# Rows that are transposed by way of DRAM and VectorE, and a start and a middle in another order, in a convolution and mixture-of-experts kernel

## The chip, the cores and the metric

The kernel runs on one core of a Trainium2 chip. Its time is the device time of one execution in microseconds (us); several executions are measured and their median is used. A profile is one execution recorded by the hardware profiler. PE is TensorE (PEld its weight loads), DVE is VectorE, ACT is ScalarE, POOL is GpSimd, and SP is the engine whose queue issues most of the transfers.

## The reference

Inputs are `x` and a context, both 8 x 256 x 512, one convolution filter of 512 taps for each of 32 heads, and the weights of a mixture of experts. Everything is float32.

```
def xattn(v, k, bias, x1, x2):                  # x1 = x2 = context
    kv = vr[:, :, :, None, :] * x2r[:, :, None, :, :]   # 8 x 8 products per head
    y  = causal_convolution(kv, k) + kv * skip          # along the 512 positions
    return einsum('bhijl,bhil->bhjl', y, x1r)
def ffn(xf):                                    # 2048 rows of 512
    scores = sigmoid(xf @ gate_w.T)             # 8 experts, the best 2 of each row
    shared = silu(xf @ shared_wg.T) * (xf @ shared_wu.T) @ shared_wd.T     # 704 wide
    routed = sum over the 2 best of 2.5 * weight * expert(xf)              # 352 wide
    return shared + routed
x = x + xattn(layernorm(x), ...)
x = x + ffn(layernorm(x), ...)
```

## The kernel before, in words

The 2048 rows are 16 tiles of 128 rows; a tile holds 16 channels of all 8 batches, which is two heads. The order of the work on every engine is written out by hand: each engine runs its instructions in the order in which the program issues them.

*Convolution stage.* The loop runs over the 32 heads `h`; `t = h // 2` is the tile. For a head, POOL makes the products `kv` (`make_kv`, two heads ahead), PE multiplies them with Toeplitz blocks of the filter (`conv_products`: ten 128x512 products into four PSUM tiles; three PSUM buffers are there), and DVE weighs each of the four results with the context and sums (`weigh(h, 0)` to `weigh(h, 3)`: a product and a reduction each). The skip term is made on POOL (`skip_products`, `skip_spread`) around a sum on DVE (`skip_sum`, `add_skip`).

`kv` needs the layer-normed tile with positions on the partitions, `vT`. DVE computes mean and variance (`stats`), ACT a square root (`rstd_of`), DVE the normed rows (`normed`); PE transposes them in four 128x128 pieces against an identity into PSUM and ACT copies them out (`transposed`, called by `make_vT`). A tile's finished sum is transposed back in the same way (`residual_T`) and added to `x` (`add_residual`). The result is normed a second time, written to DRAM as `xn_d` (for the experts' gathers later) by a transfer on SP, and transposed on PE into `xfT` (`make_xfT`), the operand of the shared expert. The odd heads do the norms of two tiles: `xn1` of tile t+2 and `xn2` of tile t-1. PE's transposes follow at the end of the same odd head.

*Shared expert and routing.* Four tiles form a chunk. Its shared products are cut into ten `steps` (six `up_step`, four `down_step`), which the head loop draws from head 10 on, one or two a head, at the end of the head; `settle` issues what they owe to DVE at the start of the next. Routing of a chunk is spread over heads: `route_logits` (PE), `route_T` (PE), `route_pick` (DVE), `route_ranks` (PE), `route_places` (DVE, then eight indirect writes on POOL into a table in DRAM).

*Tail and experts.* After the loop the last tile is normed and transposed, the last chunk is routed, the table is read back, and the remaining shared steps fill PE in between. Then 36 to 39 blocks of 128 gathered rows run through their experts. `block_T` there already brings a block into transposed form without PE: the rows are gathered in quarters, so that the 32x32-square transpose of DVE (`V.transpose`) gives a full transpose with the positions in a permuted order, and the weights' rows are permuted to match on the host.

*Start.* Tile 0 is normed, transposed, and its first `kv` made; tile 1 is normed and transposed; `kv` of head 1 and the skip products follow; then the head loop begins.

SP's queue holds all loads in program order: the Toeplitz block three heads ahead, `x` and context three tiles ahead, the residual's `x`, then whatever is written out. A transfer that waits there holds up those behind it.

Of the kernel before, what the change touches and what calls it, by code (L numbers as in the profile page):

```python
# [8 lines left out]
F32 = mybir.dt.float32  # L9
I32 = mybir.dt.int32  # L10
AF = mybir.ActivationFunctionType
ALU = mybir.AluOpType
# [28 lines left out]
Q = 32  # L41
NQ = P // Q
EPS = 1e-5
SCALE = 2.5


@with_exitstack
def tile_xattn_moe(
# [70 lines left out]
    load_toeplitz(1)  # L119


    ident = const.tile([P, P], F32, name="ident")
    make_identity(nc, ident)
    skip_sb = const.tile([P, D], F32, name="skip_sb")
# [10 lines left out]
    for e in range(NEXP):  # L135
        G.memset(rank[:, e : e + 1], float(NEXP - e))
        G.memset(base[:, e : e + 1], float(NTOK * e))
    ones = const.tile([P, P], F32, name="ones")
    G.memset(ones, 1.0)
    upper = const.tile([P, P], F32, name="upper")  # L140
    G.memset(upper, 1.0)

# [32 lines left out]


    xn_d = dram.tile([NTOK + P, L], F32, name="xn_d")
    NCOL = NEXP * CPE
    table = dram.tile([P * NCOL, 2], F32, name="table")
    zero = rows.tile([P, L], F32, tag="xg", name="zero")  # L180
# [26 lines left out]
    def rstd_of(mvs, n, m):  # L207
        r = small.tile([P, m], F32, tag="rstd", name=f"rstd{n}")
        V.tensor_scalar_add(r, mvs[:, :m, 1], EPS)
        A.activation(r, r, AF.Sqrt)  # L210
        V.reciprocal(r, r)
        return r

    def normed(tag, n, src, mv, r):
        xn = cvp.tile([P, L], F32, tag=tag, name=f"{tag}{n}", bufs=2)
        V.tensor_scalar(xn, src, mv[:, 0:1], r, ALU.subtract, ALU.mult)
        return xn

    def transposed(dst, src, n):
        pt = ps_tp.tile([P, NLB, P], F32, tag="tp", name=f"pt{n}")  # L220
        for k in range(NLB):
            T.transpose(pt[:, k, :], src[:, k * P : (k + 1) * P], ident)
        A.copy(dst, pt)  # L223
# [3 lines left out]
    def make_vT(t):  # L227
        vT[t] = cvp.tile([P, NLB, B, R], F32, tag="vT", name=f"vT_{t}")
        transposed(vT[t].rearrange("p k b r -> p k (b r)"), xn1.pop(t), f"v_{t}")

    def make_xfT(t):
        c, i = divmod(t, TPC)
        if i == 0:
            xfT[c] = shp.tile([P, NLB, TPC, P], F32, tag="xfT", name=f"xfT_{c}", bufs=2)
        transposed(xfT[c][:, :, i, :], xn2.pop(t), f"f_{t}")


    kvs = {}
# [34 lines left out]
    def weigh(h, lb, ps):  # L273
        t, cols = head_cols(h)
        if h % 2 == 0 and lb == 0:
            convT[t] = cvp.tile([P, NLB, B, R], F32, tag="conv", name=f"convT_{t}")
        prod = cvp.tile([P, B, NH, NH], F32, tag="prod", name=f"prod_{h}_{lb}", bufs=2)
        V.tensor_tensor(  # L278
            prod,
            ps,  # L280
            ctxT[t][:, lb, :, cols].unsqueeze(2).to_broadcast([P, B, NH, NH]),
            ALU.mult,
        )
        V.tensor_reduce(convT[t][:, lb, :, cols], prod, AX.X, ALU.add)  # L284
# [5 lines left out]
    def skip_products(t):  # L290
        if t >= NT:
            return
        s = cvp.tile([P, NLB, B, R], F32, tag="skip", name=f"skip_{t}")
        G.tensor_tensor(s, vT[t], ctxT[t], ALU.mult)
        flat = s.rearrange("p k b r -> p (k b) r")
        G.tensor_tensor(
            flat,
            flat,
            skip_sb[:, t * R : (t + 1) * R].unsqueeze(1).to_broadcast([P, NLB * B, R]),
            ALU.mult,  # L300
        )
        skips[t] = s

    def skip_sum(t):
        if t >= NT:
            return
        sums[t] = small.tile([P, NLB * B * 2], F32, tag="w", name=f"w_{t}")
        V.tensor_reduce(sums[t], skips[t].rearrange(BY_HEAD, i=NH), AX.X, ALU.add)

    def skip_spread(t):  # L310
        if t >= NT:
            return
        G.tensor_tensor(
            skips[t].rearrange(BY_HEAD, i=NH),
            ctxT[t].rearrange(BY_HEAD, i=NH),
            sums.pop(t).unsqueeze(2).to_broadcast([P, NLB * B * 2, NH]),
            ALU.mult,
        )
# [339 lines left out]
    def first_norms(ts):  # L658
        mv = small.tile([P, 2, V.BN_AGGR_DIM], F32, tag="mv", name=f"mvp_{ts[0]}")
        for n, t in enumerate(ts):  # L660
            stats(mv[:, n, :], f"p_{t}", x1[t])
        r = rstd_of(mv, f"p_{ts[0]}", len(ts))
        for n, t in enumerate(ts):
            xn1[t] = normed("xn1", f"_{t}", x1.pop(t), mv[:, n, :], r[:, n : n + 1])

    first_norms([0])
    make_vT(0)
    make_kv(0)
    first_norms([1])
    make_vT(1)  # L670
    make_kv(1)
    skip_products(0)

    todo = iter(steps)
    done = 0
# [1 line left out]
    def step():  # L677
        nonlocal done
        _, f, *a = next(todo)
        f(*a)  # L680
        done += 1

    def second_norm_of(t, mv, r):
        xn2[t] = normed("xn2", f"_{t}", x2[t], mv, r)
        S.dma_start(out=xn_d[t * P : (t + 1) * P, :], in_=xn2[t])

    for h in range(H):
        t, odd = divmod(h, 2)

        load_toeplitz(h + 3)  # L690
        if not odd:
            load_tile(t + 3)
            load_residual(t)
        if h == 3:
            load_shared()

        settle()
        pss = list(conv_products(h))
        weigh(h, 0, pss[0])
        ns = []  # L700
        if odd:
            skip_sum(t + 1)
            mvs = small.tile([P, 2, V.BN_AGGR_DIM], F32, tag="mv", name=f"mv_{h}")
            if t > 0:
                add_residual(t - 1)
                stats(mvs[:, len(ns), :], f"2_{t}", x2[t - 1])
                ns.append(("xn2", t - 1))
            if t + 2 < NT:
                stats(mvs[:, len(ns), :], f"1_{t}", x1[t + 2])
                ns.append(("xn1", t + 2))  # L710
            rs = rstd_of(mvs, f"_{h}", len(ns))
        else:
            if t == 0:
                skip_sum(0)
            else:
                add_skip(t - 1)
        weigh(h, 1, pss[1])
        for n, (tag, tt) in enumerate(ns):
            if tag == "xn2":
                second_norm_of(tt, mvs[:, n, :], rs[:, n : n + 1])  # L720
            else:
                xn1[tt] = normed(tag, f"_{tt}", x1.pop(tt), mvs[:, n, :], rs[:, n : n + 1])
        c, r = divmod(h - 10, 8)
        if c >= 0:
            if r == 2:
                route_pick(c)
            if r == 3:
                route_places(c)
        weigh(h, 2, pss[2])
        weigh(h, 3, pss[3])  # L730

        make_kv(h + 2)
        if not odd:
            skip_products(t + 1)
            skip_spread(t)

        if not odd and t > 0:
            residual_T(t - 1)
        if odd:
            if t > 0:  # L740
                make_xfT(t - 1)
            if t + 2 < NT:
                make_vT(t + 2)
        if c >= 0:
            if r == 0:
                route_logits(c)
            if r == 1:
                route_T(c)
            if r == 2:
                route_ranks(c)  # L750

        while done < min((h - 9) * 5 // 4, len(steps)) and steps[done][0] <= h:
            step()


    last_t, last_c = NT - 1, NCHUNK - 1
    settle()
    add_skip(last_t)
    step()
    residual_T(last_t)  # L760
    settle()
    add_residual(last_t)
    mvs = small.tile([P, 2, V.BN_AGGR_DIM], F32, tag="mv", name="mv_last")
    stats(mvs[:, 0, :], "2_last", x2[last_t])
    second_norm_of(last_t, mvs[:, 0, :], rstd_of(mvs, "_last", 1))
    step()
    make_xfT(last_t)
    conv_scope.close()
# [204 lines left out]
def _laid_out(a):  # L973

    import numpy as np

    toep = np.zeros((H, P, L), np.float32)
    for p in range(P):
        toep[:, p, p:] = a["L0_xattn_k"][:, : L - p]
    x = a["x"].reshape(B, NT, R, L).transpose(1, 0, 2, 3).reshape(NT, P, L)  # L980
    c = a["ctx_2048"].reshape(B, NT, R, NLB, P)

    g, u = a["L0_ffn_shared_wg"].T, a["L0_ffn_shared_wu"].T
    cols = [w[:, f : f + P] for f in range(0, SFF, P) for w in (g, u)]
    sgu = np.concatenate(cols, axis=1).reshape(NLB, P, 2 * SFF).transpose(1, 0, 2)
    gu = np.stack([a["L0_ffn_exp_wg"], a["L0_ffn_exp_wu"]], axis=1)

    gu = gu.reshape(NEXP, 2, FF, NQ, NLB, Q).transpose(0, 3, 5, 1, 4, 2)
    nf = len(F_TILES)
    squares = [q * nf + t for t in range(nf) for q in range(NQ) if q * nf + t < FF // Q]  # L990
    order = [s * Q + a for s in squares for a in range(Q)]
    return {
        "x": x,
        "cT": c.transpose(1, 4, 3, 0, 2),
        "toep": toep,
        "skip": a["fside_S2_0"],
        "gwT": a["L0_ffn_gate_w"].T,
        "sgu": sgu,
        "sd": a["L0_ffn_shared_wd"].T,
        "egu": gu.reshape(NEXP, P, NGU),  # L1000
        "ed": a["L0_ffn_exp_wd"].transpose(0, 2, 1)[:, order],
    }
# [24 lines left out]
```

## Time and profile before

| | us |
|---|---|
| median of 3 runs | 834.97 (834.58 to 836.86) |
| the profiled execution, whole | 848.52 |
| its span, first to last instruction | 846.8 |
| PE busy | 810.1 |
| DVE busy | 533.9 |
| POOL busy | 432.5 |
| ACT busy | 106.5 |

The profiled execution is longer than the others, so that its parts are compared with its own time. A busy PE is not PE at its peak, since matmuls overlap: the distance between starts tells what one holds of the engine. In groups of instructions, `x64` is the count, the next figures are the busy time and the mean duration. In a timeline the first figure is the start, the second the time covered, and a bracket gives the idle time before it and what ended it.

### The profile page before, as it was taken

What the parts mean: (1) busy time and instruction counts of PE and PEld (TensorE: products, weight loads), DVE (VectorE), ACT (ScalarE), POOL (GpSimd) and SP (SyncE); (2) the same over time, 40 slices, a digit from 0 to 9 for tenths busy, and PEclk for the clock granted to TensorE, in tenths of its full rate; (3) what the DMA queues carried; (4) which work ended last, traced back from release to release, by engine and by line L of the source; (5) the groups of instructions that cost most, each with busy time, mean ns of one, the idle gap of its engine ahead of it and who ended that gap; (6) DMA issues with size and microseconds to landing.
All of it is one profiled execution on the core that took longest, in us unless ns stands there. A gap on an engine that the chain in (4) does not pass through costs nothing. (4 is left out here: it accounts for less than half of the span.)

```text
span 846.8 us, 7786 instructions
## 1 busy us (share of the span) xinstructions
PE 810.1 (96%) x2247; PEld 399.2 (47%) x2247; DVE 533.9 (63%) x1340; ACT 106.5 (13%) x176; POOL 432.5 (51%) x424
## 2 busy tenths in 40 slices
PE   6999999999999999999999999979999999999991
PEld 3444444444444444444444444435555555555550
DVE  3888856657535757555555444309887788888860
ACT  1000111201011111002111010001111111111110
POOL 7965653194343074532341003762777777777521
PEclk9999999999999999999999999988999999999996
DMA  5372312201212011111000195229444444444332
GB/s 199 104 256 74 99 51 64 74 13 62 91 47 63 12 62 53 59 63 35 15 26 1 51 409 167 69 69 297 72 74 73 75 73 71 70 72 74 61 40 36
DMA packets 33418, 71.49 MB, mean 84 GB/s; under 512 B 6752, under 2 KB 7136, under 8 KB 32224
## 3 DMA queue, kind: packets, MB, share of 16 engines
q1 hardware_dynamic: 22560, 52.06, 17.9%
q0 software_dynamic: 10816, 18.92, 13.0%
q8 instruction: 20, 0.33, 0.2%
q14 instruction: 22, 0.18, 0.1%
HBM read 52.45 MB, written 18.51 MB: 84 GB/s over the span
## 5 line engine op out<-in xcount | busy, mean ns | idle before, releaser
L264 PE MATMUL cv<-kv,tz 128*128 128x512 f32 x640 | 282.3, 596 | 0.0
L250 POOL TENSOR_TENSOR kv<-vT,ctxT 128x512 f32<-128x512 f32 x128 | 134.8, 1085 | 146.8 <-ACT vT L223 117.6
L264 PEld LDWEIGHTS cv<-kv,tz 128*128 128x128 f32 x640 | 121.3, 191 | 150.8 <-issue 136.9
L861 PE MATMUL up<-wgu_sb,xT 128*128 (+1 forms) x576 | 180.1, 465 | 6.9 <-issue 3.8
L802 POOL DMA_INDIRECT xg<-xn_d,src x144 | 146.8, 1019 | 57.5 <-issue 42.1
L474 PE MATMUL gu<-xfT,wsh 128*128 128x512 f32 x352 | 156.7, 600 | 0.0
L905 DVE STREAM_TRANSPOSE hTb<-h 32x96 f32<-32x96 f32 (+1 forms) x560 | 146.3, 261 | 8.2
L861 PEld LDWEIGHTS up<-wgu_sb,xT 128*128 128x128 f32 x576 | 110.4, 192 | 80.2 <-issue 22.3
L278 DVE TENSOR_TENSOR prod<-cv,ctxT 128x512 f32<-128x512 f32 x128 | 87.4, 683 | 36.4 <-PE cv L264 36.0
L446 POOL DMA_INDIRECT table<-entry,to x32 | 31.8, 994 | 140.7 <-DVE at L442 132.1
L474 PEld LDWEIGHTS gu<-xfT,wsh 128*128 128x128 f32 x352 | 66.1, 192 | 79.4 <-issue 79.2
L919 PE MATMUL y<-wd_sb,hTb 128*128 (+3 forms) x216 | 98.6, 593 | 0.8 <-ACT hTb L894 0.8
L284 DVE TENSOR_REDUCE convT<-prod 128x64 f32<-128x512 f32 x128 | 87.8, 686 | 4.4
L928 POOL DMA_INDIRECT out_dram<-ys,row x36 | 58.2, 1616 | 55.7 <-ACT ys L927 32.8
L519 PE MATMUL dn<-wshd,hT 128*128 128x512 f32 x160 | 70.6, 593 | 0.0
L919 PEld LDWEIGHTS y<-wd_sb,hTb 128*128 128x128 f32 (+1 forms) x216 | 41.0, 190 | 43.1 <-issue 34.9
L491 DVE TENSOR_TENSOR sg<-sg,gu 128x512 f32<-128x512 f32 (+1 forms) x24 | 16.4, 685 | 65.5 <-ACT sg L488 65.5
L544 DVE TENSOR_TENSOR x<-dn,x 128x512 f32<-128x512 f32 x16 | 10.4, 687 | 62.8 <-PE dn L532 45.6
L519 PEld LDWEIGHTS dn<-wshd,hT 128*128 128x128 f32 x160 | 29.6, 190 | 34.2 <-issue 34.2
L870 DVE TENSOR_TENSOR h<-h,up 128x352 f32<-128x352 f32 x36 | 18.6, 517 | 39.5 <-ACT h L869 22.6
L869 ACT ACTIVATE h<-up 128x352 f32<-128x352 f32 x36 | 16.6, 463 | 192.7 <-PE up L861 167.9
L493 DVE TENSOR_TENSOR hT<-sg,gu 128x512 f32<-128x512 f32 x20 | 13.8, 688 | 36.2 <-PE gu L474 33.9
(122 smaller groups left out, 410.5 us busy)
## 6 DMA issues: line engine op xcount, KB each, us to landing
wgu_sb<-in_egu_dram SPq DMA_DIRECT2D x8, 1408.0 KB
x<-in_x_dram SPq DMA_DIRECT2D x32, 256.0 KB
tz<-in_toep_dram SPq DMA_DIRECT2D x32, 256.0 KB
ctxT<-in_cT_dram SPq DMA_DIRECT2D x16, 256.0 KB
xn_d<-xn SPq DMA_DIRECT2D x16, 256.0 KB
out_dram<-x SPq DMA_DIRECT2D x16, 256.0 KB
wd_sb<-in_ed_dram SPq DMA_DIRECT2D x8, 512.0 KB
wsh<-in_sgu_dram SPq DMA_DIRECT2D x1, 2816.0 KB
```

The source lines that it names most:

```text
L250: G.tensor_tensor(kv[:, mb], vT[t][:, mb, :, cols].unsqueeze(2).to_broadcast([P, B, NH, NH]), ctxT[t][:, mb, :, cols].unsqueeze(3).to_broa ...
L264: T.matmul(ps.rearrange("p b j i -> p (b j i)"), lhsT=tz[:, (lb - mb) * P : (lb - mb + 1) * P], rhs=kv[:, mb].rearrange("p b j i -> p (b j ...
L278: V.tensor_tensor(prod, ps, ctxT[t][:, lb, :, cols].unsqueeze(2).to_broadcast([P, B, NH, NH]), ALU.mult,)
L284: V.tensor_reduce(convT[t][:, lb, :, cols], prod, AX.X, ALU.add)
L446: ins = G.indirect_dma_start(out=table, out_offset=bass.IndirectOffsetOnAxis(ap=to[:, i : i + 1], axis=0), in_=entry[:, i, n, :], in_offse ...
L474: T.matmul(ps, lhsT=wsh[:, k, m0 : m0 + m], rhs=rhs[k], start=(k == 0), stop=(k == NLB - 1))
L519: T.matmul(ps, lhsT=hTs[c][:, ft, i * P : (i + 1) * P], rhs=wshd[:, ft, :], start=(ft == 0), stop=False,)
L802: G.indirect_dma_start(out=xgs[k][:, c, :], out_offset=None, in_=xn_q, in_offset=bass.IndirectOffsetOnAxis(ap=src[:, c, k : k + 1], axis=0 ...
L861: T.matmul(ps[:, m, :FF], lhsT=xTs[k][:, j].rearrange("p c b -> p (c b)"), rhs=wk[:, bass.ds(eks[k] * NGU + (m * NLB + j) * FF, FF)], star ...
L905: V.transpose(hT[q * Q : (q + 1) * Q, :n, c], hk[c * Q : (c + 1) * Q, q * NF * Q : (q * NF + n) * Q].rearrange("p (t a) -> p t a", a=Q),)
L919: T.matmul(ps, lhsT=hT[:fw, ft].rearrange("p c b -> p (c b)"), rhs=wk[:fw, bass.ds(eks[k] * NWD + ft * L, L)], start=(ft == 0), stop=(ft = ...
L928: G.indirect_dma_start(out=out, out_offset=bass.IndirectOffsetOnAxis(ap=row[:, k : k + 1], axis=0), in_=y, in_offset=None, bounds_check=NT ...
```

## The change

- The transposes of the normed rows leave PE, except for tiles 0 and 1 on the way in and tile 15 on the way out. ACT norms the rows (as `rstd * x + nb`, with `nb = -mean * rstd` from DVE), ACT's queue writes them to DRAM (`xv_d` for the first norm, `xn_d` for the second), SP loads them back in four quarters, each onto 32 partitions (`quarters`), and DVE transposes 32x32 squares (`squares_T`). For the first norm ACT writes the positions in an order that undoes the permutation; for the second the rows of `gwT` and `sgu` are permuted on the host (`by_quarter`).
- The loads are issued in the odd head; DVE takes them up in the next even head, after `weigh(h, 1)`.
- The transfer of `xn_d` moves from SP's queue to ACT's.
- The shared steps come ahead of `residual_T`, `route_logits`, `route_T` and `route_ranks` on PE. `route_ranks` and `route_places` come one head later.
- `skip_sum` moves behind `weigh(h, 2)`, `skip_spread` ahead of `make_kv`.
- At the start, six 128x256 products of constants run on PE ahead of everything (`warm`); their operands are set first on POOL. Tile 1's transpose goes behind head 0's products, and `skip_products(0)` ahead of `kv` of head 1.

```
@@ start
+    ones = const.tile([P, P], F32, name="ones")
+    G.memset(ones, 1.0)
+    filler = rows.tile([P, 2 * P], F32, tag="xg", name="filler")
+    G.memset(filler, 0.0)
...
     first_norms([0])
+    warm = ps_gu.tile([P, 2 * P], F32, tag="gu", name="warm")
+    for _ in range(WARM):
+        T.matmul(warm, lhsT=ones, rhs=filler, start=True, stop=True)
     make_vT(0)
     make_kv(0)
     first_norms([1])
-    make_vT(1)
+    skip_products(0)
     make_kv(1)
-    skip_products(0)
@@ norms
+        nb = small.tile([P, 2], F32, tag="nb", name=f"nb{n}")
+        V.scalar_tensor_tensor(nb[:, :m], mvs[:, :m, 0], -1.0, r, ALU.mult, ALU.mult)
...
-        V.tensor_scalar(xn, src, mv[:, 0:1], r, ALU.subtract, ALU.mult)
+        A.activation(xn, src, AF.Identity, scale=rb[0], bias=rb[1])
@@ the way to transposed form
+    def quarters(key, rows_d):
+        xq[key] = cvp.tile([P, NQ, P], F32, tag="xq", name=f"xq_{key[0]}{key[1]}", bufs=3)
+        for q in range(NQ):
+            S.dma_start(
+                out=xq[key][q * Q : (q + 1) * Q],
+                in_=rows_d[:, q * P : (q + 1) * P].rearrange("(c b) m -> b c m", b=Q),
+            )
+    def squares_T(dst, key):
+        V.transpose(
+            dst.rearrange("p k (c b) -> p c k b", b=Q),
+            xq.pop(key).rearrange("p c (k a) -> p c k a", a=Q),
+        )
+    def first_norm(t, rb):
+        xn = cvp.tile([P, NQ, NLB, Q], F32, tag="xn1", name=f"xn1_{t}", bufs=2)
+        normed(xn, x1.pop(t).rearrange("p (k s a) -> p s k a", s=NQ, a=Q), rb)
+        A.dma_start(out=xv_d[t], in_=xn.rearrange("p s k a -> p (s k a)"))
+    def second_norm(t, rb):
+        xn = cvp.tile([P, L], F32, tag="xn2", name=f"xn2_{t}", bufs=2)
+        normed(xn, x2[t], rb)
+        A.dma_start(out=xn_d[t * P : (t + 1) * P, :], in_=xn)
+        if t < NT - 1:
+            return
+        xn2[t] = cvp.tile([P, NLB, NQ, Q], F32, tag="xn1", name="xn2_kqa", bufs=2)
+        A.copy(xn2[t], xn.rearrange("p (q k a) -> p k q a", q=NQ, a=Q))
@@ head loop
-            skip_sum(t + 1)
...
         weigh(h, 1, pss[1])
-        for n, (tag, tt) in enumerate(ns):
...
+        if not odd and t > 0:
+            if t + 1 < NT:
+                square_vT(t + 1)
+            if t > 1:
+                square_xfT(t - 2)
+        for (tag, tt), rb in sorted(zip(ns, rs or ()), key=lambda n: n[0]):
+            (second_norm if tag == "xn2" else first_norm)(tt, rb)
+        for tag, tt in sorted(ns):
+            if tag == "xn1":
+                quarters(("v", tt), xv_d[tt])
             else:
+                quarters(("f", tt), xn_d[tt * P : (tt + 1) * P, :])
...
-            if r == 3:
+            if r == 4:
                 route_places(c)
         weigh(h, 2, pss[2])
+        if odd or h == 0:
+            skip_sum(t + odd)
         weigh(h, 3, pss[3])
+        if h == 0:
+            make_vT(1)
+        if not odd:
+            skip_spread(t)
         make_kv(h + 2)
         if not odd:
             skip_products(t + 1)
-            skip_spread(t)
+        while done < min((h - 9) * 5 // 4, len(steps)) and steps[done][0] <= h:
+            step()
         if not odd and t > 0:
             residual_T(t - 1)
-        if odd:
-            if t > 0:
-                make_xfT(t - 1)
-            if t + 2 < NT:
-                make_vT(t + 2)
...
-            if r == 2:
+            if r == 3:
                 route_ranks(c)
-        while done < min((h - 9) * 5 // 4, len(steps)) and steps[done][0] <= h:
-            step()
@@ tail
     add_skip(last_t)
+    square_xfT(last_t - 1)
     step()
@@ host: the order of the positions in two weights
+    def by_quarter(w):
+        return w.reshape(NQ, NLB, Q, -1).transpose(1, 0, 2, 3).reshape(L, -1)
...
-        "gwT": a["L0_ffn_gate_w"].T,
+        "gwT": by_quarter(a["L0_ffn_gate_w"].T),
```

## The prediction

> **What bounds the kernel now.** I read the page's busy shares first, then the groups by line and shape, then the table by 20 us stage, then the timelines of the start and of one early pair of heads.
>
> ```profile
> span 846.8 us, 7786 instructions
> PE 810.1 (96%) x2247; PEld 399.2 (47%) x2247; DVE 533.9 (63%) x1340; ACT 106.5 (13%) x176; POOL 432.5 (51%) x424
> ```
> TensorE is busy all but 36.7 us. By stage:
>
> ```profile
> 0.00:20.00 20.00, 12.11 (x27) 5.98 (x28) 6.72 (x15) 2.83 (x5) 15.68 (x48) 1.00 0.61 211
> 60.00:80.00 20.00, 20.00 (x57) 9.45 (x56) 16.80 (x31) 1.30 (x3) 13.73 (x13) 1.00 0.23 79
> 120.00:140.00 20.00, 19.76 (x56) 9.36 (x55) 11.84 (x22) 3.18 (x5) 7.66 (x7) 1.00 0.21 67
> 560.00:580.00 20.00, 13.06 (x31) 7.01 (x30) 9.74 (x29) 0.99 (x3) 6.06 (x6) 0.74 0.56 184
> ```
> The first figure after the length is PE, the third DVE, the fifth POOL. From 20 to 540 us PE is full in nearly every row; DVE reaches 84% in the heads before the shared steps and some 60% later. So in the conv stage a PE instruction removed is time removed, if nothing else comes late. What a set of four transposes holds of PE:
>
> ```profile
> 47.83 0.60 PE L222 MATMUL ptf<-ident,xn 128*128 128x128 f32 x4
> 48.27 0.60 PE L222 MATMUL ptv<-ident,xn 128*128 128x128 f32 x4
> 48.70 8.75 PE L264 MATMUL cv<-kv,tz 128*128 128x512 f32 x20
> 57.29 0.60 PE L329 MATMUL ptr<-ident,convT 128*128 128x128 f32 x4
> ```
> Durations overlap; starts count: 0.435 us from one set to the next. A head's 20 conv records (each 128x512 f32 product is two) take 8.59, so 0.43 each. The start is different:
>
> ```profile
> 5.78 1.09 PE L222 MATMUL ptv<-ident,xn 128*128 128x128 f32 x4 [5.78 <-DVE xn L216]
> 8.98 1.12 PE L222 MATMUL ptv<-ident,xn 128*128 128x128 f32 x4 [2.11 <-DVE xn L216]
> 9.89 19.45 PE L264 MATMUL cv<-kv,tz 128*128 128x512 f32 x40
> 12.45 0.34 PEld L264 LDWEIGHTS cv<-kv,tz 128*128 128x128 f32 x1 [0.52 <-POOL kv L250]
> 13.30 0.34 PEld L264 LDWEIGHTS cv<-kv,tz 128*128 128x128 f32 x1 [0.52 <-issue]
> 14.15 0.19 PEld L264 LDWEIGHTS cv<-kv,tz 128*128 128x128 f32 x1 [0.51 <-issue]
> 14.58 0.19 PEld L264 LDWEIGHTS cv<-kv,tz 128*128 128x128 f32 x1 [0.24 <-issue]
> ```
> Up to 14.15 a conv record takes 0.85 us, afterwards 0.43: half clock, although the stage table says 1.00. And conv begins only at 9.89, behind tile 1's transposes.
>
> The rows that step 4 below rests on, DVE's spare time in an even head first:
>
> ```profile
> 57.49 0.69 DVE L278 TENSOR_TENSOR prod<-cv,ctxT 128x512 f32<-128x512 f32 x1 [2.02 <-PE cv L264]
> 483.75 0.33 SPq L685 DMA_DIRECT2D xn_d<-xn  x1
> 485.93 4.35 SPq L772 DMA_DIRECT2D wgu_sb<-in_egu_dram  x8
> SPq L772 <- DMA xn_d<-xn: 1.7, 1, 1.7
> 526.06 0.33 SPq L607 DMA_DIRECT2D tab<-table  x1
> 528.11 0.43 DVE L625 COPY by_quarter<-tab 128x512 f32<-128x512 f32 x1 [0.64 <-DMA tab<-table]
> ```
>
> **The change, part by part** (minus is gained)
>
> 1. *Transposes off PE.* 14 sets for vT (tiles 2 to 15) and 15 for xfT (tiles 0 to 14) go: 29 x 0.435 = **-12.6 us**. The Trainium skill, page "TensorE: Matmul & The Clock Gate", section "Part 4: PE-mode transpose", gives about 275 ns for one 128x128 transpose and says that such work does not get the full clock: 116 x 0.275 = 31.9 us. The profile's duration agrees (273 ns), but the starts are 0.109 apart and the conv behind runs at full rate; I keep 12.6.
>
> 2. *What DVE takes over.* Per pair of heads it loses two normalisations (L216, about 0.5 each) and gains two 32x32-square transposes and one tiny product for the bias. The square transpose of the expert blocks (L823) has the same shape and takes 0.711, the tiny product about 0.17: +0.6. DVE's 15.5 us of an 18.5 us pair become 16.1 of 17.6 (91%). The low end of the unknown is 0.71; the high one is 1.25, what L321 takes beside POOL (17.2 of 17.6). I take 0.71, the nearest row, and +0.7 for lateness in the four or five early pairs. With shared steps behind every head from the 11th on, a pair is over 28 us and DVE has room.
>
> 3. *ACT* loses 29 copies of 0.585 and gains 32 normalisations (bound 0.585 from those copies, 0.687 from L927, which also scales) and 30 DMA issues (0.33 as on SP). It is 13% busy; its square roots wait for DVE. Zero, hidden by PE; without that cover some 0.3 us a tile. Should the new function need a table load (1.283 us each in this trace), a pair's rows come 2.6 us later, which only the early pairs would feel.
>
> 4. *The round trip through DRAM.* New: 14 writes of xv_d, 116 quarter loads on SP; the 16 writes of xn_d move from SP to ACT. A write costs at most 2.2 us (xn_d issued at 483.75, its waiter on SP goes at 485.93), a load about 2.05 (the table, 526.06 to 528.11), a load's issue 0.33 to 0.43. Count from R, when the reciprocal is done in an odd head, 5.5 us after its conv begins: bias 0.2, v normed R+0.85, v written R+3.1, four issues to R+4.7, v landed R+6.4; f normed R+1.9, written R+4.2, issued behind v to R+6.3, landed R+8.0. DVE asks for v 12.8 us after that conv's start, R+7.3, and for f at R+8.0. It just fits in the early pairs; later each head carries at least 4.3 us of shared steps more. If DVE waits, weigh(h,2) and (h,3) queue behind it; the three conv banks let PE go on about 2 us. The skill's page "DMA: Bandwidth & Descriptors", section "Measured (HBM→SBUF, 128 partitions, SWDGE, issued from GpSimd)", warns that transfers under 64 KB are descriptor-dominated and gives 0.95 us for 64 KB. Eight quarters in single file at that price bring f to about R+11.7: 3.7 late, some 2 us lost in each of four early pairs, 8 in all. The row for a 128 KB load, 2.05 from issue to use, includes the latency, so I do not stack them; I take nothing and keep 8 for the range. On SP the quarters' wait stands ahead of the next Toeplitz, x, context and residual loads, by some 4 us; those are issued three heads (26 us) early. POOL's kv(h+2) starts after the squares: about 11 us ahead of its conv.
>
> 5. *Start.* kv(0) follows tile 0 alone: normed by ACT about 0.3 later, transposed in 0.45 instead of 1.09, so kv's first quarter is ready at 8.2 rather than 8.6 and conv(0) starts at 8.25. The six warming products need only two memsets, so PE works from 1.3 to about 6.2. Conv(0) ends at 16.9, vT(1) adds 0.43, conv(1) ends at 25.9 instead of 29.34: **-3.4**. kv(1), now behind skip_products(0), is there at 15.0 for 17.3. Half of the gain is the clock: before, it took 5.2 us of steady work (8.98 to 14.15) to open; the warming lasts 5.1 and a gap under 2 us follows. If it stays shut, 2.1 comes back.
>
> 6. *Small work behind the steps, ranks a slot later.* Before, PE waits 0.41 for plT and 0.33 for the ranks in each of three chunks, and 0.4 for one ptv: **-2.2**. The scatters move a head later on POOL, whose kv has a head's slack. The earlier skip_spread puts 1.1 us ahead of kv on POOL, hidden by the same slack; skip_sum moves behind weigh 2, so R comes 0.7 earlier.
>
> 7. *Tail.* For tile 15 ACT norms, issues the write, then copies once more: 485.0 against 484.4, when PE is free: **+0.7**. The stretch 560 to 572, where PE, DVE, ACT and SP all stall together, is code that the change leaves alone; it can shift by 1 or 2 either way.
>
> Sum: -12.6 +0.7 -3.4 -2.2 +0.7 = **-16.8**. The profiled execution (848.5 us, span 846.8) would come to about 831.7; it stands 13.5 above the median of the runs, and since the steps are engine times I take the same difference off the median: 834.97 - 16.8 = 818.2.
>
> **Rivals.**
> *A: late quarters or a full DVE in the early heads.* For it: 91% and zero margin for f; against it: 84% now, with 2 us of DVE idle before weigh(h,3) in even heads. It costs 4 to 8: 822 to 826.
> *B: the clock stays cold at the start and some waits stay.* +2 to +3: about 821.
> *C: better than summed:* DVE delays nothing, ACT makes the tail no later: 814 to 817.
> *D: slower.* The quarters land so late that PE waits in every pair. The place is the squares in each even head; 15 of them must each lose 1.3 us to bring PE to 838. That needs f to land about 3 us beyond DVE's turn in the early pairs (R+11) and beyond R+16 or more in the later ones, a round trip of double the 8 us worked out. The only loads near that size take 2 us here, DMA is 0.2 busy; against it also that the late pairs have most of the room.
> *E: no net change.* The same, with some 1.1 us lost in each pair.
>
> **How the numbers follow.** Forecast 0.56 (816 to 820), C 0.10, B 0.12, A 0.15, E 0.03, D 0.04. Range 813.5 to 826: it takes in B, C, A and the +-2 of the stall. About 0.3% (2.5 us) is what a measurement of this kernel can tell from no change: faster 0.93, same 0.03, slower 0.04.
>
> **What would show it.** PE records fall by 116 and rise by the warming ones; head-to-head distance in the early heads goes to 8.6 with 0.43 more every second head; the conv records' starts are 0.43 apart from the first head on; conv(1) ends near 26; L355 and L413 sit right behind the shared products. The DVE square transposes show whether they wait for the DMA: waits over 2 us in the early even heads mean A, in all of them D or E. If the DVE transposes take 1.2 us, step 2 was wrong; if PE still has gaps before the conv of odd heads, step 4 was.

## The result and the profile after

The changed kernel takes 826.91 us (median of 4 runs, 824.95 to 829.57) against 835.0 for the kernel before: ratio 0.9888, 95% interval 0.9868 to 0.9908. It is faster by about 8 us, half of the 16.8 forecast. The profiled execution took 827.25 us.

The page of the changed kernel, span and engine totals:

```profile
span 825.5 us, 7804 instructions
PE 796.1 (96%) x2143; PEld 388.2 (47%) x2143; DVE 565.2 (68%) x1356; ACT 117.1 (14%) x180; POOL 429.3 (52%) x425
```

PE has 104 records fewer: 116 of transposes gone, 12 of warming products added. The span is 21.3 us shorter, more than the runs show. About half of that comes behind the first expert product, where the profile of before had PE at 13.06 of 20 us (560 to 580) and this one has it at 20.00. That difference is no work of this change (last section), so the two profiles are compared up to the first expert product: it starts at 554.37 before and at 544.59 after, 9.8 us earlier.

The table by stage of the changed kernel (columns as before: length, then PE, PEld, DVE, ACT and POOL busy with counts, clock, DMA share, GB/s):

```profile
40.00:60.00 20.00, 16.30 (x40) 7.23 (x39) 13.03 (x24) 1.83 (x3) 10.44 (x11) 0.96 0.84 291
60.00:80.00 20.00, 20.00 (x49) 8.93 (x48) 18.65 (x32) 1.83 (x3) 12.36 (x13) 0.95 0.37 119
140.00:160.00 20.00, 18.61 (x47) 8.23 (x46) 18.88 (x40) 2.11 (x3) 10.71 (x10) 1.00 0.05 13
560.00:580.00 20.00, 20.00 (x62) 11.44 (x61) 19.02 (x64) 2.99 (x5) 11.43 (x10) 1.00 0.91 230
```

Two rows of the conv stage have lost what they had before: 40 to 60, with DVE at 13.03 and DMA at 0.84, and 140 to 160, with DVE nearly full. The same rows of the kernel before:

```profile
40.00:60.00 20.00, 20.00 (x57) 9.52 (x56) 16.81 (x30) 1.31 (x3) 13.64 (x14) 1.00 0.89 315
140.00:160.00 20.00, 19.85 (x53) 9.11 (x52) 14.36 (x45) 2.11 (x3) 0.00 (x0) 1.00 0.05 14
```

The timeline of the changed kernel around head 4:

```profile
36.19 0.44 SPq L195 DMA_DIRECT2D wsh<-in_sgu_dram  x1
43.07 0.33 ACTq L257 DMA_DIRECT2D xv_d<-xn  x1
50.58 1.76 SPq L242 DMA_DIRECT2D xq_v<-xv_d  x4
53.66 1.02 PE L312 MATMUL cv<-kv,tz 128*128 128x512 f32 x2
54.02 0.71 DVE L248 STREAM_TRANSPOSE vT<-xq_v 128x512 f32<-128x512 f32 x1 [4.03 <-DMA xq_v<-xv_d]
57.05 0.71 DVE L248 STREAM_TRANSPOSE xfT<-xq_f 128x512 f32<-128x512 f32 x1 [2.32 <-DMA xq_f<-xn_d]
58.39 18.26 PE L312 MATMUL cv<-kv,tz 128*128 128x512 f32 x38 [3.70 <-DVE prod L326]
```

ACT issues the write of the rows at 43.07; the quarters that read them leave SP only at 50.58. DVE waits twice, the weighing behind it waits, and PE stands still for 3.70 us and then works a part of the 38 records at half clock: from 53.66 to the next transpose at 76.49 are 22.83 us for 40 records of 0.43 (17.2), so 5.6 are lost. What held the write is in the DMA view of 36 to 58 us (KB of each, then median us from issue to landing):

```profile
wsh<-in_sgu_dram SPq DMA_DIRECT2D x1, 2816.0 KB, 9.4
wshd<-in_sd_dram SPq DMA_DIRECT2D x1, 1280.0 KB, 14.7
xv_d<-xn ACTq DMA_DIRECT2D x1, 256.0 KB, 7.4
xq_v<-xv_d SPq DMA_DIRECT2D x4, 64.0 KB, 2.0
```

The shared expert's weights (`load_shared` in head 3, over 4 MB) are on the way, and a 256 KB write takes 7.4 us instead of 2.0, its median over the whole kernel. The second place, timeline of the changed kernel in head 12:

```profile
141.23 4.13 POOL L298 TENSOR_TENSOR kv<-vT,ctxT 128x512 f32<-128x512 f32 x4 [11.00 <-PE cv L312]
142.38 0.98 DVE L430 TENSOR_TENSOR key<-score,top 128x32 f32<-128x32 f32 x1
143.40 0.99 DVE L431 TENSOR_TENSOR key<-key,rank 128x32 f32<-128x32 f32 x1
144.42 0.19 DVE L432 TENSOR_REDUCE best<-key 128x4 f32<-128x32 f32 x1
151.05 1.00 DVE L438 TENSOR_SCALAR den<-den 128x4 f32<-128x4 f32 x1
154.39 7.99 PE L312 MATMUL cv<-kv,tz 128*128 128x512 f32 x18 [1.40 <-DVE prod L326]
286.50 7.99 PE L312 MATMUL cv<-kv,tz 128*128 128x512 f32 x18 [1.40 <-DVE prod L326]
418.60 7.99 PE L312 MATMUL cv<-kv,tz 128*128 128x512 f32 x18 [1.63 <-DVE prod L326]
```

`vT` comes from the square transpose in the even head now, so POOL starts `kv` there, and `route_pick`, which follows on DVE, runs beside it. Its small instructions with two inputs take 0.8 to 1.2 us; before, with POOL idle, 0.15 to 0.2, as in this line of the kernel before:

```profile
143.55 0.19 DVE L382 TENSOR_TENSOR key<-score,top 128x32 f32<-128x32 f32 x1
```

The pick lasts 12 us (141.6 to 153.6) instead of 4.9 (142.8 to 147.6), and PE waits for the weighing, once in each of the three chunks: 4.4 us of gaps.

### The profile page after: what moved, and what is told of

The parts are those of the page before. It is cut to its first block, busy times and chain, and to the rows that moved or that the text cites. A ratio compares the mean times of both kernels' runs of the same rounds, so it can differ in the third digit from the quotient of the medians.

```text
span 825.5 us, 7804 instructions
## 1 busy us (share of the span) xinstructions
PE 796.1 (96%) x2143; PEld 388.2 (47%) x2143; DVE 565.2 (68%) x1356; ACT 117.1 (14%) x180; POOL 429.3 (52%) x425
## 5 line engine op out<-in xcount | busy, mean ns | idle before, releaser
L312 PEld LDWEIGHTS cv<-kv,tz 128*128 128x128 f32 x640 | 119.6, 191 | 158.9 <-issue 125.2
L298 POOL TENSOR_TENSOR kv<-vT,ctxT 128x512 f32<-128x512 f32 x128 | 132.4, 1067 | 92.8 <-PE cv L312 76.9
L914 PE MATMUL up<-wgu_sb,xT 128*128 (+1 forms) x576 | 176.1, 459 | 0.0
L522 PE MATMUL gu<-xfT,wsh 128*128 128x512 f32 x352 | 154.4, 593 | 0.0
L361 POOL TENSOR_TENSOR skip<-ctxT,w 128x512 f32<-128x512 f32 x16 | 17.7, 1108 | 47.7 <-DVE w L356 47.7
L536 ACT ACTIVATE sg<-gu 128x512 f32<-128x512 f32 (+1 forms) x24 | 14.3, 596 | 178.6 <-PE gu L522 178.5
```

The source lines that it names most:

```text
L298: G.tensor_tensor(kv[:, mb], vT[t][:, mb, :, cols].unsqueeze(2).to_broadcast([P, B, NH, NH]), ctxT[t][:, mb, :, cols].unsqueeze(3).to_broa ...
L312: T.matmul(ps.rearrange("p b j i -> p (b j i)"), lhsT=tz[:, (lb - mb) * P : (lb - mb + 1) * P], rhs=kv[:, mb].rearrange("p b j i -> p (b j ...
L522: T.matmul(ps, lhsT=wsh[:, k, m0 : m0 + m], rhs=rhs[k], start=(k == 0), stop=(k == NLB - 1))
L914: T.matmul(ps[:, m, :FF], lhsT=xTs[k][:, j].rearrange("p c b -> p (c b)"), rhs=wk[:, bass.ds(eks[k] * NGU + (m * NLB + j) * FF, FF)], star ...
```

## The experiments

The runs were made in four groups, each against runs of the kernel before beside it. In one group that kernel took 836.76 us, in the others 847.74, 849.2 and 849.47; a standstill in the experts' stage, shown in the last section, goes with this. So ratios are formed within a group, and a second measure is free of that stage: the time from the conv's first product to tile 15's transpose on PE, read off each timeline. It is 474.5 for before (9.89 to 484.38; 474.5 in its two other profiles too) and 467.7 for after (9.33 to 477.05).

| kernel | median us | before beside it | ratio (95% interval) | conv to tile 15 |
|---|---|---|---|---|
| shared_behind | 837.21 | 847.74 | 0.987 (0.9855 to 0.9885) | 465.2 |
| pick_first | 833.82 | 847.74 | 0.9837 (0.9824 to 0.9851) | 463.0 |
| both | 831.37 | 847.74 | 0.9813 (0.98 to 0.9827) | 459.8 |
| after_again | 827.36 | 836.76 | 0.9905 (0.9882 to 0.9927) | 468.4 |
| spread_pick | 816.23 | 836.76 | 0.9773 (0.9755 to 0.9792) | 456.9 |
| back_on_pe | 833.79 | 836.76 | 0.9974 (0.9961 to 0.9987) | 472.1 |
| no_warm | 830.76 | 836.76 | 0.9946 (0.9925 to 0.9967) | 470.0 |
| start_alone | 850.38 | 849.2 | 1.0018 (1.0011 to 1.0025) | 478.8 |
| steps_alone | 856.9 | 849.2 | 1.0088 (1.0075 to 1.0101) | 484.1 |
| steps_sum | 849.69 | 849.47 | 0.9994 (0.9978 to 1.001) | 473.6 |

**The two losses, one at a time and together**

`shared_behind`: the weights are issued behind the quarters of head 3.

```
-        if h == 3:
-            load_shared()
         settle()
...
+        if h == 3:
+            load_shared()
         weigh(h, 2, pss[2])
```

> The changed kernel with the shared expert's weights (4.3 MB) issued on SP behind the quarters of head 3 instead of ahead of them. Theory Q (the quarters of head 3 land late because 4.3 MB stand before them on the transfers): DVE's square transposes of head 4 don't wait, PE's 3.7 us gap near 55 us and the half clock behind it go: 5 to 5.6 us faster than the changed kernel, about 821. Rival (the rows themselves come too late in early heads, whatever else is loaded): the wait in head 4 stays at 2 us or more and similar ones show in heads 6 and 8; gain under 1 us.

`pick_first`: the pick goes ahead of the square transposes, so before POOL can start.

```
         weigh(h, 1, pss[1])
+        c, r = divmod(h - 10, 8)
+        if c >= 0 and r == 2:
+            route_pick(c)
         if not odd and t > 0:
             if t + 1 < NT:
                 square_vT(t + 1)
...
-            if r == 2:
-                route_pick(c)
```

> The changed kernel with route_pick ahead of the two square transposes in its head, so that POOL's kv starts only after it. DVE has exactly the same work. Theory P (POOL's kv, now started in the same even head, slows the small DVE instructions of route_pick from 0.19 to about 1 us each): route_pick takes about 5 us instead of 12, PE's three gaps of 1.4 to 1.6 us and what follows are gone, 4 to 4.5 us faster, about 822.5. Rival (DVE simply has too much in that head since the transposes came): the gaps stay, no change.

`both` has the two edits together.

> Both edits together: weights behind the quarters, route_pick ahead of the squares. If the two losses are separate they add: 9 to 10 us faster than the changed kernel, about 817, where the prediction had put it (818.2). If one is the other's cover, less than 7 us.

Against after's 467.7, the measure falls by 2.5, 4.7 and 7.9 us: the two add, within the 0.7 by which after's own two profiles differ. Moving the weights gave half of the 5 to 5.6 expected, and so the two together less than the 9 to 10. The pick's loss went as its theory has it; timeline of `pick_first`, the same instructions:

```profile
141.16 0.19 DVE L430 TENSOR_TENSOR key<-score,top 128x32 f32<-128x32 f32 x1
141.38 0.19 DVE L431 TENSOR_TENSOR key<-key,rank 128x32 f32<-128x32 f32 x1
143.47 0.17 DVE L438 TENSOR_SCALAR den<-den 128x4 f32<-128x4 f32 x1
```

Nothing of the pick is changed but its place, and POOL's `kv` now begins behind it (146.19). The three gaps of PE are gone. Head 4's loss only moved: a little more than half came back, in head 6 and behind it. Timeline of `both`:

```profile
48.96 0.43 SPq L195 DMA_DIRECT2D wsh<-in_sgu_dram  x1
58.44 0.33 SPq L104 DMA_DIRECT2D ctxT<-in_cT_dram  x1
61.58 0.33 ACTq L257 DMA_DIRECT2D xv_d<-xn  x1
66.05 0.33 SPq L115 DMA_DIRECT2D tz<-in_toep_dram  x1
67.31 1.75 SPq L242 DMA_DIRECT2D xq_v<-xv_d  x4
70.85 0.71 DVE L248 STREAM_TRANSPOSE vT<-xq_v 128x512 f32<-128x512 f32 x1 [2.36 <-DMA xq_v<-xv_d]
73.93 7.99 PE L312 MATMUL cv<-kv,tz 128*128 128x512 f32 x18 [1.53 <-DVE prod L326]
```

SP's own issues are far apart now (58.44, 66.05), and the quarters stand behind them in its queue: the rows' write is issued at 61.58, the quarters only at 67.31. The profile puts SP's wait before 58.44 down to the landing of `wsh` (6.2 us) and the next one down to that of `wshd` (3.7). So the weights have to be thinned out, not moved.

`spread_pick`: `pick_first`, and the weights in pieces, one every second head.

```
     def load_shared():
-        S.dma_start(out=wsh, in_=sgu)
...
-        if h == 3:
+        if h in (2, 4, 6, 8):
+            S.dma_start(out=wsh[:, h // 2 - 1], in_=sgu[:, h // 2 - 1])
+        if h == 10:
             load_shared()
```

> The changed kernel with route_pick ahead of the squares, and the shared weights in pieces: 0.7 MB each at heads 2, 4, 6 and 8, the down weights at head 10. Theory Q (the bulk of 4.3 MB in SP's queue is what holds the quarters up, ahead of them in head 4, or behind them by way of the loads of head 5 in head 6): no wait of DVE for quarters above 1 us in any even head, 9.5 to 10.5 us faster than the changed kernel. Rival (early heads have no room for the round trip in any case): waits of 1 to 2 us in heads 4, 6, 8 remain, gain no more than the 7.9 us that both edits gave up to the last tile's transpose.

816.23 us, 2.3% under the kernel before, the best version found. Its PE timeline in the early heads:

```profile
35.54 17.33 PE L311 MATMUL cv<-kv,tz 128*128 128x512 f32 x40
53.15 17.33 PE L311 MATMUL cv<-kv,tz 128*128 128x512 f32 x40
```

A pair of heads takes 17.61 us from one to the next, as the prediction had it, and PE has no gap from 8.81 to 465.70. In the head loop no DVE transpose waits more than 0.26 us for its quarters: those that start on time are in time in the early heads too.

`after_again` is the changed kernel once more, beside these.

> The changed kernel again, as the reference for the other runs of this set. Its ratio to the kernel before was 0.9888. If the stretch in the experts' first blocks in which four engines stand still (10 to 14 us in the second profile of the kernel before and in all edits run beside it) belongs to the chip, it is in this profile too, although the first profile of this same kernel had none, and the ratio stays within 0.986 to 0.991. If it belongs to the kernel before alone, this profile has none.

Its ratio agrees with the first one.

**What the transposes bring, and what start and order bring without them**

`back_on_pe`: everything of the change but the way through DRAM. ACT norms, PE transposes both kinds of rows at the end of the odd head as before, and the positions are in plain order.

```
-                square_vT(t + 1)
...
-                square_xfT(t - 2)
...
         if not odd and t > 0:
             residual_T(t - 1)
+        if odd:
+            if t > 0:
+                make_xfT(t - 1)
+            if t + 2 < NT:
+                make_vT(t + 2)
...
     def by_quarter(w):
-        return w.reshape(NQ, NLB, Q, -1).transpose(1, 0, 2, 3).reshape(L, -1)
+        return w
```

> The changed kernel with all transposes of normed rows on PE again, at the end of the odd head as before (rows still normed and written by ACT, shared weights in plain order, no quarters, no square transposes); start, order of the steps and slots stay as changed. By the sum of the prediction the transposes are worth 12.6 less 0.7 and 0.7: 11 us slower than the changed kernel. By the reading of the profiles (5.6 us lost in head 4 and 4.5 in three route_picks come with them) only 2 us slower, with no PE gap in head 5 and route_pick at 0.19 us an instruction.

`no_warm`: no warming products.

```
-WARM = 6
+WARM = 0
```

> The changed kernel without the six warming products. If they open the clock: conv starts at 9.3 us as before or up to 0.2 earlier, its first five to ten records take 0.85 us instead of 0.43, 1.5 to 3 us slower. If the clock opens late anyway, no difference.

Without the way through DRAM the rest of the change gains only 0.3%. From `back_on_pe` to the changed kernel are 6.4 us of median (833.79 - 827.36), and to `spread_pick` 17.6 us, or 15.2 by the second measure: this is about the 12.6 of step 1 and the small waits which `back_on_pe` still has (two of 0.79 for a `ptv`, five of 0.24 for `plT` and the ranks). So neither size expected of `back_on_pe` was met (11, or 2 by the losses): the transposes are worth more than 11, and the two losses take most of it back.

The warming products are worth 3.4 us of median, with intervals that just touch (0.9882 to 0.9927 against 0.9925 to 0.9967); in the profiles tile 15's transpose comes 2.0 to 2.2 us later without them (479.23 against 477.22 and 477.05). PE timeline of `no_warm`, then of `after_again`:

```profile
9.19 11.23 PE L312 MATMUL cv<-kv,tz 128*128 128x512 f32 x20 [1.82 <-POOL kv L298]
```

```profile
6.37 0.63 PE L226 MATMUL ptv<-ident,xn 128*128 128x128 f32 x4 [0.30 <-ACT xn L221]
8.82 10.41 PE L312 MATMUL cv<-kv,tz 128*128 128x512 f32 x20 [1.82 <-POOL kv L298]
58.56 18.27 PE L312 MATMUL cv<-kv,tz 128*128 128x512 f32 x38 [2.82 <-DVE prod L326]
```

Without the warming products the first conv takes 11.23; with them it takes 8.85 in the changed kernel's first profile and in six other profiles, but 10.41 in `after_again`.

`start_alone`: the kernel before with the new start only (warming, tile 1's transpose behind head 0, `skip_products(0)` ahead of `make_kv(1)`, `skip_sum(0)` behind `weigh(0, 2)`).

```
+    for _ in range(WARM):
+        T.matmul(warm, lhsT=ones, rhs=filler, start=True, stop=True)
     make_vT(0)
     make_kv(0)
     first_norms([1])
-    make_vT(1)
-    make_kv(1)
     skip_products(0)
+    make_kv(1)
...
         weigh(h, 2, pss[2])
+        if h == 0:
+            skip_sum(0)
         weigh(h, 3, pss[3])
+        if h == 0:
+            make_vT(1)
```

> The kernel before with only the start changed: warming products, tile 1's transpose behind head 0's products, skip_products(0) ahead of kv of head 1, skip_sum(0) behind weigh(0, 2). The prediction's sum has 3.4 us faster; the start of the changed kernel's profiles (conv of head 1 ends at 26.5 to 27.1 instead of 29.3) says 2.3 to 2.8. Here DVE norms, 0.3 us sooner than ACT would: 2.5 to 3 us faster. Rival: the clock opens at the same time anyway, 1 us.

`steps_alone`: the kernel before with the shared steps ahead of PE's small work, ranks and places a head later.

```
-            if r == 3:
+            if r == 4:
                 route_places(c)
...
+        while done < min((h - 9) * 5 // 4, len(steps)) and steps[done][0] <= h:
+            step()
         if not odd and t > 0:
             residual_T(t - 1)
...
-            if r == 2:
+            if r == 3:
                 route_ranks(c)
-        while done < min((h - 9) * 5 // 4, len(steps)) and steps[done][0] <= h:
-            step()
```

> The kernel before with only the order changed: shared steps ahead of PE's small work, ranks and places one head later. The prediction's sum has 2.2 us faster (0.41 and 0.33 us of PE's idle time in each of three chunks and less). If the transposes at the end of the odd head, now behind the steps, make vT and with it POOL's kv late, PE waits for kv and the kernel is no faster or slower.

A gain was expected of both (2.5 to 3 and 2.2 us); both lose. Timeline of `start_alone`:

```profile
24.86 0.69 DVE L311 TENSOR_REDUCE w<-skip 128x64 f32<-128x512 f32 x1 [5.11 <-POOL skip L299]
29.36 1.09 PE L225 MATMUL ptv<-ident,xn 128*128 128x128 f32 x4 [3.35 <-DVE xn L219]
```

The 3.5 us are won (conv of head 1 ends at 25.85 instead of 29.34), and given back at once: `skip_sum` is ahead of the norms on DVE and waits for POOL, the norms come late, and PE waits for them with tile 2's transpose. The same on `steps_alone`, where the scatters of `route_places` (183.95 to 194.1) push the skip products back on POOL:

```profile
199.59 1.26 POOL L296 TENSOR_TENSOR skip<-skip,skip_sb 128x512 f32<-128x512 f32 x1
200.88 0.69 DVE L308 TENSOR_REDUCE w<-skip 128x64 f32<-128x512 f32 x1 [6.39 <-POOL skip L296]
207.23 0.95 PE L222 MATMUL ptf<-ident,xn 128*128 128x128 f32 x4 [3.10 <-DVE xn L216]
```

`steps_sum` tests that reading: `steps_alone`, and `skip_sum` moved behind `weigh(h, 2)`.

```
         if odd:
-            skip_sum(t + 1)
...
         weigh(h, 2, pss[2])
+        if odd:
+            skip_sum(t + 1)
         weigh(h, 3, pss[3])
```

> The kernel before with the shared steps ahead of TensorE's small work and ranks and places a head later, as in steps_alone (ratio 1.0088), and one thing more: skip_sum stands behind weigh(h, 2) in the odd heads instead of ahead of the norms. Theory: in steps_alone the eight scatters fall into an even head, push skip_products late on POOL, and DVE's skip_sum, which waits for them, holds up the norms and so PE's transposes; behind weigh(h, 2) the norms no longer wait. Expected: the two waits of 3.10 and 2.86 us of ptf for xn in front of the conv behind the ranks fall below 1 us, with them the half-clock stretch behind them; from conv's first product to tile 15's transpose 474 us or less (before 474.5, steps_alone about 485); ratio 0.994 to 1.000. Rival: the order of the steps itself is what costs (the norms are late because DVE owes the shared steps' work): the waits stay at 3 us, 480 us or more, ratio 1.005 or more.

Both waits, 3.10 and 2.86, are gone. Timeline of `steps_sum`, at the same place as the first:

```profile
200.41 2.17 DVE L216 TENSOR_SCALAR xn<-x,mv,rstd 128x512 f32<-128x512 f32 x2
203.18 0.60 PE L222 MATMUL ptf<-ident,xn 128*128 128x128 f32 x4
203.82 0.68 DVE L308 TENSOR_REDUCE w<-skip 128x64 f32<-128x512 f32 x1
```

From 484.1 to 473.6 us by the second measure, and from 1.0088 to 0.9994: one reduction in its right place is worth 10 us in that order. The order itself then gains 0.9 us at most on the kernel before, since the short waits for ACT's copies (0.24) and two of 0.79 remain.

Two runs of the kernel before, unchanged, were made for their profiles:

> The kernel before, profiled a second time. Theory S: the stretch from 560 to 572 us in the first profile, in which PE, DVE, ACT and SP all stand still and PE's clock falls to half, belongs to that one execution: this profile has a span near 833 us and PE full there. Theory T: it belongs to the kernel before: the span is again near 847 us, the stall is there again, and then the change has removed it.

> The kernel before, profiled a third time. If the standstill of four engines in the experts' first blocks belongs to the chip and not to the kernel, then on a chip where the kernel before takes about 835 us its profile has none and a span near 834, with the same times as the other profiles up to the first expert product (552 to 554 us).

They took 847.53 and 848.17 us; what they show stands in the last section.

## Why the prediction was right in direction, and double in size

The mechanism was right: a PE instruction removed from the conv stage is time removed. The terms of the sum held, or nearly so, and two waits that it counted at nothing took 10 us of it. At 826.9 the kernel stands at the slow end of the range (826).

*Step 1, -12.6:* held. PE's pairs are 17.61 apart in `spread_pick` and 18.48 in `back_on_pe` (45.23 to 63.71): 0.87, two sets of 0.435. The 0.275 of one transpose in the Trainium skill (page "TensorE: Matmul & The Clock Gate", section "Part 4: PE-mode transpose") would have made the difference 2.2.

*Step 2, what DVE takes over:* the sizes held and the step failed. The square transposes take 0.70 in the median and 0.71 at most, and DVE is 91% busy at 80 to 100 (18.25 of 20), as forecast; the 0.7 of lateness did not come, since PE has no gap in `spread_pick`. But the step only summed DVE's time. It had the line of a DVE instruction slowed beside POOL (L321, 1.25) and weighed it for the transposes alone. It did not ask what DVE's other instructions run beside once `kv` starts in the even head; `route_pick` became two and a half times as long, and PE lost 4.4 us in gaps, 4.7 by `pick_first`. The pick is not the only place: the small addition ahead of the square root (L213) takes 0.98 in the mean of 13 odd heads, for 0.17 before, without holding up PE. The Trainium skill, page "SBUF — State Buffer", section "SBUF: two separate sides", has a rule that should have been weighed here: VectorE and GpSimd share a pair of ports, which is locked for a whole instruction when VectorE reads two tensors from SBUF or runs in a two-port mode. The trace agrees: two-input instructions and the `TENSOR_SCALAR` go from 0.15 to 0.2 up to 0.8 to 1.2, about one `kv` quarter (1.03), and the reduction between them stays at 0.19.

*Step 3, ACT, 0:* held. The bias product takes 0.55 where 0.2 was put, and ACT's norm 0.81 where 0.687 was the bound, so the write is issued some 0.6 us later than counted (43.07, where R is 41.6); `spread_pick` shows that the early heads had room for it.

*Step 4, the round trip, 0:* right in its durations, wrong in its surroundings. In an undisturbed head the quarters leave 2.1 us behind the write (24.02 to 26.11, forecast 2.2) and land in 2.0 (median of 56; 1.9 to 2.3, forecast 2.05). The step asked what the quarters hold up in SP's queue, and not what holds them up. `load_shared` stood in head 3 before as well, where nothing short of time shared the queues with it; it was not counted, and cost 5.6 us. The prediction took the DMA engines as 0.2 busy, and the row of before in which these weights are loaded (40 to 60, shown above) has them at 0.89. Rival A had named the early heads and 4 to 8 us for them, but with a cause (no room in any of them, DVE full) that `spread_pick` refutes. That A's price and the end of the range were about met is chance. The Trainium skill, page "DMA: Bandwidth & Descriptors", section "Issuing engines are not separate DMA queues", says that transfers share the same 16 DMA engines whichever engine issues them: sending the write from ACT does not take it past SP's bulk load, as the 7.4 us show.

*Step 5, the start, -3.4:* -2.3 in the first profile of the changed kernel, -1.2 in `after_again`, -2.8 in `spread_pick` (end of conv(1), before at 29.34). PE timeline of the changed kernel, start, and step 7's place:

```profile
1.33 5.49 PE L719 MATMUL warm<-filler,ones 128*128 128x256 f32 x12 [1.33 <-POOL filler L126]
6.61 0.89 PE L226 MATMUL ptv<-ident,xn 128*128 128x128 f32 x4
9.33 8.85 PE L312 MATMUL cv<-kv,tz 128*128 128x512 f32 x20 [1.82 <-POOL kv L298]
18.45 8.75 PE L312 MATMUL cv<-kv,tz 128*128 128x512 f32 x20
...
477.05 0.66 PE L226 MATMUL ptf<-ident,xn_kqa 128*128 128x128 f32 x4 [0.71 <-ACT xn_kqa L271]
```

The clock is open for conv(0), as forecast, though not in `after_again`; tile 0's transpose still runs partly at half of it, and ACT's norm takes 0.81 us. Conv(0) starts at 9.33 instead of 8.25 and conv(1) ends at 27.0 instead of 25.9. With DVE's norm (`start_alone`) the two are 8.14 and 25.85.

*Step 6, -2.2:* the waits it names are gone; by its own figures they add to 2.6 (three times 0.41 and 0.33, and 0.4). The runs showed a condition that it gave as a small gain: `skip_sum` behind `weigh(h, 2)` is what lets order and start pay at all. So the steps are not additive: order and start alone cost 0.9% and 0.2%, together with that move (and the norms on ACT, in `back_on_pe`) they gain 0.3%. The start with the move alone was not run.

*Step 7, +0.7:* 0.71, as the last line shows. The 13.5 us that the sum carried over to the median was right to be carried: it belongs to the profiled run of before, and after's profiled run stands at its median.

The sum to tile 15's transpose with the measured sizes: -12.6 -2.3 -2.6 +0.7, and -1.1 for two waits of 0.57 for `xn` in the profile of before (200.17 and 335.26), which the prediction left out, make -17.9. With +5.6 and +4.4 for the two new waits it is -7.9; the timelines show -7.3 (484.38 to 477.05). Without the new waits, and with the -2.8 of its start, `spread_pick` comes to -18.4; its timeline shows -18.7 (484.38 to 465.70). Between tile 15's transpose and the first expert product the changed kernel gained another 2.4, which is not attributed: three profiles of before differ by 2 us there themselves.

## What to carry to other kernels

When work leaves the bound engine for a chain of transfers and a second engine, list what else is in the queues and on the ports at every place where the chain runs, once-only loads included: the chain was sized right here, and its two costs came from a bulk load and from an engine that now started at the same time as some small instructions. A wait at the head of an in-order queue is worth moving before anything is hung behind it; the same reorderings lost 0.9% with `skip_sum` ahead of the norms and nothing with it behind.

## What the runs showed of the hardware

*A standstill that goes with the group of runs.* PE, DVE and ACT stand still in the experts' first blocks, while POOL's gathers go on: in the 30 us behind the first expert product PE is idle for 6.4 to 9.7 us, and its granted clock, in steps of 10 us, falls to 0.60 to 0.74. This is so in the profile of before that the prediction used and in every profile of the groups in which the kernel before takes over 847 us, whichever kernel runs. In both profiles of the changed kernel and in the others of the group with 836.76 PE is idle for 0.00 us there. From the waits of the first profile of before (total us, times, longest):

```profile
DVE x L544 <- remote: 14.4, 1, 14.4
```

And the stage table of `before_again`, to be compared with the full row of after:

```profile
560.00:580.00 20.00, 10.61 (x26) 5.77 (x25) 9.81 (x31) 1.28 (x3) 5.67 (x6) 0.74 0.72 209
```

It goes with the 13 us between 835 and 848. Each of the four groups ran on a chip of its own, so the chip may be what it goes with. The prediction took it for a part of the code that could shift by 1 or 2 us. Its cause was not tried and stays open; nor is there a profile of the kernel before from a group without it.

*The clock closes after gaps of about 3 us, and near the edge one gap can go both ways.* Behind gaps of 3.70, 3.35, 3.10 and 2.82 us PE's records take up to twice their time for a while (the last is the third line of `after_again`); behind those of 1.40 to 1.74 they do not (`154.39 7.99`: 18 records of 0.43). The gap of 1.82 ahead of conv(0) stands in all eight profiles with warming products: in seven conv(0) runs at full rate, in `after_again` its first records take twice their time (10.41 against 8.85). What decides there was not tried. The Trainium skill, page "TensorE: Matmul & The Clock Gate", section "Part 1: The HAM clock gate (the "warmup" mystery)", gives an idle window of about 3.4 us; 2.82 was enough here. The clock column shows 0.96 where it closed. The warming products took 5.44 to 5.49 us in four profiles and 4.46 to 4.74 in four others.
